# The last down projection of a hybrid attention kernel: exact 12-bit parts in place of float32

## The chip, the core and the metric

One core of one Trainium2 chip runs the whole kernel in one launch. The metric is the device time of the launch in microseconds; the median of some runs is given. The core has five engines that run side by side, each with its own queue of instructions that it takes in order: TensorE (PE, the matrix unit; PEld is its weight load), VectorE (DVE), ScalarE (ACT), GpSimd (POOL) and SyncE (SP, which here only issues DMAs). Tiles live in SBUF; matmuls write to PSUM, which has eight banks of 128 partitions by 512 float32.

## The reference

The input `x` has 4 images of 512 rows by 256 columns. Three layers run one after the other, each adding to `x`:

- Layer a, a windowed attention. An image is seen as 8192 tokens of 16 channels on a grid of 128 by 64; query, key and value come from a 16x48 matrix. Half of the channels attend in windows of 1x8, half in windows of 8x1, each with a depthwise 3x3 convolution added, then a projection, a layer norm and the residual.
- A feed-forward layer (called f below): layer norm over 256 columns, then `down(gelu(gate(x)) * up(x))` with 2048 hidden units, and the residual.
- Layer b, a causal attention with 16 heads of 16 over the 512 rows, with rotary embedding; then the same feed-forward layer again (called s below), with the same weights, and the residual.

The gate, up and down weights are 4-bit codes with scales, two codes in a word, dequantised once in the kernel to float32.

## The kernel before

The work of one feed-forward pass over one image is the unit to keep in mind: f0 to f3 and s0 to s3. The hidden units go through in 16 chunks of 128. For each chunk `n` TensorE makes a gate tile `pg` and an up tile `pu` (128 hidden units by 512 rows, one PSUM bank each), ScalarE applies the gelu, VectorE multiplies them to `it`, and after eight chunks (a `half`) the down projection runs: for each of 4 groups `i` of 128 rows, eight float32 matmuls of 256 columns into a bank `po`, which VectorE adds to the image's tile `X[b]`.

From f2 on, gate and up products don't run in float32. Each operand is split into a high part of 12 bits and a rest; `keep_parts` writes three forms of the gate and up weights (high; the rest; a third one for the correction) to a tensor in device memory, `kept`. For each weight tile ScalarE makes three scaled copies (`less`, `high`, `low`), SP stores them, and GpSimd issues two accumulating DMAs that add a tile onto what was stored: a first stage `kept<-raw` onto the `less` form, and two turns later a second stage `kept<-kept`, which reads what the first stage left. So each turn is three activations, three stores and two accumulating DMAs. Then a gate or up tile takes four products in a fast float32 form, a scaling of the bank by 1 + 2^-12 on ScalarE, and two more products onto it (`begin` and `end`). The chunks come back from `kept` by one DMA of 768 KB each (`chunk_f`, `chunk_s`).

What sets the order:

- The first part (windowed attention of the four images, f0 to f2) is woven by hand: `weave` takes steps of a feed-forward pass and of the window work beside it. It holds TensorE's order, and in the weave of f1 GpSimd's; the other engines' instructions are placed by the framework's scheduler, which may put them earlier than written. `beside_window(2)` is the window work of image 2, beside f1, with `keep_parts` in between; `beside_window(3)` stands beside f2. Each ends with `norm_rows`, which makes the normed and turned rows `xT` of the next feed-forward pass; its `inv_root` runs on GpSimd and gives `rs_f`.
- The second part (causal attention of the four images, f3 and s0 to s3) is ordered by a planner, the class `Conductor`: every step has an engine, a cost in us and a rank, and the planner writes out all engines' orders. `RANK`, `BOOST` and the number given to `run` are its tuning. s3 stands alone at the end, as nothing is left to run beside it.
- PSUM: two double banks (`pair`), and in the first part one bank `one` and three banks `fbank` (tag `ps`), in the second part four `ps`.

Of the kernel before, what the change touches and what calls it, by code (L numbers as in the profile page):

```python
# [18 lines left out]
P = 128  # L19
# [20 lines left out]
def hybrid_kernel(  # L40
# [47 lines left out]
    X = [const.tile([P, 4, W], F32, name=f"X{b}") for b in range(B)]  # L88
# [19 lines left out]
    store = ctx.enter_context(tc.tile_pool(name="store", bufs=1, space=bass.MemoryType.DRAM))  # L108
    kept = [store.tile([4, P, 2, 3, 2, P], F32, name=f"kept{q}") for q in range(4)]
# [852 lines left out]
    def down(b, name, half, inter, last, later=None):  # L962
        for i in range(4):
            if later:
                later.room()
            po = fbank.tile([P, 512], F32, tag="ps", name=f"po_{name}_{half}_{i}")
# [34 lines left out]
    def keep_parts(pool):  # L1001

        of = lambda t: t.rearrange("p (n c) -> p n c", c=P)
        turns = [(q, k, mat, par) for q in range(4) for k, mat in enumerate("gu") for par in range(2)]

        def home(at, form):
            q, k, _, par = turns[at]
            return kept[q][:, :, k, form, par, :].rearrange("n p c -> p n c")

        for at in range(len(turns) + 4):  # L1010
            if at < len(turns):
                q, k, mat, par = turns[at]
                w = Wf[mat][par][q]
                less = pool.tile([P, 512], F32R, tag="g2", name=f"less_{mat}{par}_{q}")
                high = pool.tile([P, 512], F32R, tag="gu", name=f"high_{mat}{par}_{q}")
                nc.scalar.activation(less, w, AF.Copy, scale=-NEAR)
                nc.sync.dma_start(out=home(at, 1), in_=of(less.bitcast(F32)))
                nc.scalar.activation(high, w, AF.Copy, scale=NEAR)
                nc.sync.dma_start(out=home(at, 0), in_=of(high.bitcast(F32)))
                low = pool.tile([P, 512], F32, tag="g2", name=f"low_{mat}{par}_{q}")  # L1020
                nc.scalar.activation(low, high.bitcast(F32), AF.Copy, scale=-STEP)
                nc.sync.dma_start(out=home(at, 2), in_=of(low))
            if 0 <= at - 2 < len(turns):
                q, k, mat, par = turns[at - 2]
                nc.gpsimd.dma_start(out=home(at - 2, 1), in_=of(Wf[mat][par][q]), accum_op=ALU.add)
            if 0 <= at - 4:
                nc.gpsimd.dma_start(out=home(at - 4, 2), in_=home(at - 4, 1), accum_op=ALU.add)
            yield 0.0

# [11 lines left out]
    def ffn_in_parts(pool, ipool, ring, b, xT, name, tanh, last):  # L1041

        xs = in_parts(ring, xT, name)
        chunks = {}

        def begin(mat, n):
# [3 lines left out]
            ps = fbank.tile([P, 512], F32, tag="ps", name=f"p{mat}_{name}_{n}")  # L1050
# [14 lines left out]
        for half in range(2):  # L1065
# [38 lines left out]
            for _ in down(b, name, half, inter, last):  # L1104
                yield 0.86
# [21 lines left out]
    HOLD, BOOST = 0.25, 6.1  # L1127

    class Conductor:
# [9 lines left out]
            max=-2.21, oT=1.96, gu=0.59, add=4.1, parts=2.85, norm_s=-1.04, inv=-2.33, qb=1.22, v=1.99,  # L1139
            straight=2.4, sum=-0.69, norm_b=3.15, cube=3.78, it=8.4, plane=1.98, exp=3.03, scale=-1.64, copy=1.69,  # L1140
            gelu=0.87, square=2.39, tanh=2.67,
# [133 lines left out]
    def conduct(ring, got3, got_b0):  # L1275
# [67 lines left out]
        def ffn_pass(b, name, xT, tanh, last):  # L1343
# [33 lines left out]
            def end(mat, n):  # L1377
# [27 lines left out]
                else:  # L1405
                    gs, g2 = tiles.pop(("gate", n))
                    it = inter[n] = Slot(II, [P, 512], F32, "it", f"it_{name}_{n}")
                    if tanh:
                        gu = Slot(PF, [P, 512], F32, "gu", f"gu_{name}_{n}")
# [4 lines left out]
                    else:  # L1414
                        step("DVE", 0.69, lambda: nc.vector.tensor_tensor(it(), ps(), gs(), ALU.mult),
                             r=[ps, gs], w=[it], new=[it], lane="ffn", rank="gu")

            def down(half, i):
# [14 lines left out]
                final = b == B - 1 and last and half == 1 and i == 3  # L1433
                parts = 2 if final else 1
                for n in range(parts):
                    at = slice(n * W // parts, (n + 1) * W // parts)
                    step("DVE", 0.42 / parts, lambda at=at: nc.vector.tensor_tensor(X[b][:, i, at], po()[:, at], X[b][:, i, at], ALU.add),  # L1437
                         r=[po], w=[("X", b, i)], lane="ffn", rank="add")
                    if last and half == 1:
                        step("ACT" if n else "SP", 0.06,  # L1440
                             lambda at=at, n=n: (nc.scalar if n else nc.sync).dma_start(out=out[b, i * P : (i + 1) * P, at], in_=X[b][:, i, at]),
                             r=[("X", b, i)], lane="ffn", rank=6)

            seq = [(mat, n) for n in range(16) for mat in ("g", "u")]
            held = None
            for k, (mat, n) in enumerate(seq):
                if (mat, n) == ("g", 8):
# [11 lines left out]
                held = mat, n  # L1459
            end(*held)  # L1460
# [7 lines left out]
        def consts():  # L1468
# [9 lines left out]
            sq = [bc.tile([P, 4, HEADS, 32], F32, name=f"sq{i}") for i in range(2)]  # L1478
            sk = [bc.tile([P, HEADS, 32], F32, name=f"sk{i}") for i in range(4)]
            V = bc.tile([P, 4, HEADS, 32], F32, name="V")  # L1480
# [113 lines left out]
        qT = bc.tile([P, 4, 512], F32, name="qT")  # L1594
        kT = bc.tile([P, 4, 512], F32, name="kT")
# [311 lines left out]
    with ExitStack() as left:  # L1907
# [216 lines left out]
        def beside_window(b):  # L2124
# [8 lines left out]
            yield from between(beside, keep_parts(f1) if b == 2 else iter(()))  # L2133
# [22 lines left out]
        weave(ffn_in_parts(f1, i1, wraw, 2, got[2], "f2", False, False), beside_window(3), 1.0)  # L2156
# [4 lines left out]
    with tc.manual_schedule(  # L2161
# [5 lines left out]
        conduct(ring, got[3], mine[0]).run(0.068)  # L2167
# [88 lines left out]
```

## Time and profile before

| | us |
|---|---|
| median of 3 runs | 993.89 (990.49 to 994.48) |
| the profiled execution, its own time | 989.58 |
| its span in the profile | 987.9 |
| TensorE busy | 950.0 (96%) |
| VectorE busy | 698.5 (71%) |
| ScalarE busy | 489.6 (50%) |
| GpSimd busy | 178.7 (18%) |

A row of the profile has the line in the code, the engine, the operation, what it writes and reads by the program's names, the shapes and a count. In a timeline the first two numbers are the start and the length in us; in brackets stands the idle time of the engine before the row and what ended it. A float32 matmul stands as two records, a product from parts as one. TensorE's records overlap, because matmuls are pipelined, so the cost of one is read from start to start. f1 runs from about 187 to 285 us, f2 from there to 373 us, and s3 from 912 us to the end. TensorE's clock is granted in full nearly everywhere (mean 0.991).

### The profile page before, as it was taken

How to read it: one execution, taken by the hardware profiler on the slowest of the kernel's cores; microseconds unless marked ns; L12 is line 12 of the kernel's file. 1: busy time of each engine (PE TensorE's matmuls, PEld its weight loads, DVE VectorE, ACT ScalarE, POOL GpSimd, SP SyncE). 2: the span in 40 equal slices, each digit the busy share in tenths (PEclk: the TensorE clock that was granted, in tenths of full speed). 3: DMA queues.
4: the chain of work that ended last, by engine and by line, in shares of the span. 5: the costliest groups of instructions: out<-in, count | busy, mean ns of one | idle time of the engine just before them, and what ended most of it. 6: DMA issues, size and time to landing. Idle time of an engine off the chain costs nothing.

```text
span 987.9 us, 15864 instructions
## 1 busy us (share of the span) xinstructions
PE 950.0 (96%) x5936; PEld 662.5 (67%) x5936; DVE 698.5 (71%) x1598; ACT 489.6 (50%) x872; POOL 178.7 (18%) x295
## 2 busy tenths in 40 slices
PE   8989998899999999899999999999999999999998
PEld 6864657555677776666566666676666667657887
DVE  8999996889794868865876676667776667556211
ACT  4562277541334423565462853737717648475531
POOL 2100000078200024111422123111141111120000
PEclk9999998999999999999999999999999999999999
DMA  5320147799916325421220330522503406134730
GB/s 144 97 66 22 64 116 203 208 120 194 155 47 209 128 60 201 137 89 65 97 97 1 128 129 7 187 75 83 185 1 128 139 15 220 35 133 139 255 126 31
DMA packets 70975, 111.92 MB, mean 113 GB/s; under 512 B 5682, under 2 KB 55114, under 8 KB 70866
## 3 DMA queue, kind: packets, MB, share of 16 engines
q1 hardware_dynamic: 52000, 101.92, 31.7%
q0 software_dynamic: 16992, 8.44, 7.2%
q8 instruction: 47, 0.77, 0.3%
q10 hardware_dynamic: 1906, 0.54, 0.3%
q14 instruction: 30, 0.25, 0.1%
HBM read 92.01 MB, written 23.07 MB: 116 GB/s over the span
## 4 chain that ended last, share of the span: by engine, by line
PE 76%; DVE 12%; ACT 5%; DMA 3%; issue 1%; SPq 1%; POOL 0%; DVEq 0%; ACTq 0%
PE po_s L1425 11%; PE pg_s L1369 6%; PE pu_s L1369 6%; PE pg_f L925 5%; PE pu_f L946 5%; PE s L1640 5%; PE po_f L974 4%; PE sT L1674 4%; PE o L1718 3%; PE pu_s L1382 3%; PE po_f L1425 3%; PE qk_b L1553 3%; PE pg_s L1382 3%; PE v_b L1585 2%; PE pg_f L1369 2%; DMA chunk_f<-kept 1%
## 5 line engine op out<-in xcount | busy, mean ns | idle before, releaser
L1654 DVE CUSTOM_DVE_ANT_0 junk<-s,mask 128x512 f32<-128x512 f32 (+3 forms) x256 | 125.6, 491 | 54.3 <-PE s L1640 20.7
L1425 PE MATMUL po_s<-d,it_s 128*128 128x256 f32 x512 | 117.7, 382 | 0.6 <-DVE it_s L1412 0.5
L1693 POOL TENSOR_SCALAR_AFFINE_SELECT e<-e 128x256 f32<-128x256 f32 x128 | 53.4, 429 | 340.0 <-ACT e L1686 314.2
L1425 PEld LDWEIGHTS po_s<-d,it_s 128*128 128x128 f32 x512 | 95.2, 190 | 20.5 <-issue 5.2
L1686 ACT ACTIVATE e<-sT 128x1024 f32<-128x1024 f32 (+1 forms) x66 | 64.7, 1006 | 88.7 <-PE sT L1674 88.6
L974 PE MATMUL po_f<-d,it_f 128*128 128x256 f32 x384 | 86.4, 381 | 1.0 <-DVE it_f L1091 0.6
L974 PEld LDWEIGHTS po_f<-d,it_f 128*128 128x128 f32 x384 | 71.8, 190 | 12.6 <-issue 1.1
L1369 PE MATMUL pg_s<-xs_s,chunk_s 128*128 128x512 f32 x256 | 71.5, 401 | 0.5 <-ACT qT L1617 0.5
L1369 PE MATMUL pu_s<-xs_s,chunk_s 128*128 128x512 f32 x256 | 71.3, 400 | 0.5 <-DVE gu_s L1410 0.5
L1369 PEld LDWEIGHTS pu_s<-xs_s,chunk_s 128*128 128x128 f32 x256 | 47.6, 190 | 18.2 <-issue 1.7
L1374 ACT ACTIVATE pu_s<-pu_s 128x512 f32<-128x512 f32 x64 | 37.3, 583 | 42.1 <-PE pu_s L1369 41.2
L1369 PEld LDWEIGHTS pg_s<-xs_s,chunk_s 128*128 128x128 f32 x256 | 47.5, 190 | 14.9 <-ACT qT L1617 1.3
L937 ACT ACTIVATE gs_f<-pg_f 128x512 f32<-128x512 f32 x32 | 19.0, 594 | 73.9 <-PE pg_f L925 71.0
L1640 PE MATMUL s<-kT,qT 16*128 16x256 f32 (+3 forms) x512 | 50.9, 468 | 3.2 <-ACT qT L1617 1.9
L1374 ACT ACTIVATE pg_s<-pg_s 128x512 f32<-128x512 f32 x64 | 37.3, 583 | 22.1 <-PE pg_s L1369 21.6
L1396 DVE SCALAR_TENSOR_TENSOR g_s<-g_s,gs_s 128x512 f32<-128x512 f32 x48 | 33.6, 701 | 20.5 <-ACT g_s L1394 20.5
L1718 PE MATMUL o<-e,V 128*32 128x256 f32 (+3 forms) x512 | 44.4, 442 | 0.0
L1410 DVE SCALAR_TENSOR_TENSOR gu_s<-pu_s,gs_s 128x512 f32<-128x512 f32 x48 | 33.0, 689 | 14.7 <-PE pu_s L1382 13.9
L1382 PE MATMUL pu_s<-xs_s,chunk_s 128*128 128x512 f32 x128 | 41.8, 408 | 1.1 <-ACT pu_s L1374 1.1
L1382 PE MATMUL pg_s<-xs_s,chunk_s 128*128 128x512 f32 x128 | 41.8, 408 | 0.3 <-ACT pg_s L1374 0.3
L1437 DVE TENSOR_TENSOR X<-po_s,X 128x256 f32<-128x256 f32 (+1 forms) x33 | 13.3, 413 | 35.9 <-PE po_s L1425 35.9
L946 PE MATMUL pu_f<-xT_f,raw 128*128 128x512 f32 x80 | 38.6, 594 | 0.0
(317 smaller groups left out, 1951.4 us busy)
## 6 DMA issues: line engine op xcount, KB each, us to landing
chunk_s<-kept SPq DMA_DIRECT2D x64, 768.0 KB
chunk_f<-kept SPq DMA_DIRECT2D x32, 768.0 KB
kept<-kept POOLq DMA_DIRECT2D x16, 256.0 KB, 6.9
kept<-raw POOLq DMA_DIRECT2D x9, 256.0 KB, 7.8
X<-in_x_dram SPq DMA_DIRECT2D x4, 512.0 KB
kept<-less_g SPq DMA_DIRECT2D x8, 256.0 KB
kept<-high_g SPq DMA_DIRECT2D x8, 256.0 KB
kept<-low_g SPq DMA_DIRECT2D x8, 256.0 KB
```

The costliest lines, as they stand in the source:

```text
L925: nc.tensor.matmul(pg, Wf["g"][par][q][:, o : o + P], xT[:, par, :], start=par == 0, stop=par == 1)
L946: nc.tensor.matmul(pu, Wf["u"][par][q][:, o : o + P], xT[:, par, :], start=par == 0, stop=par == 1)
L974: nc.tensor.matmul(po[:, 0:W], inter[k][:, i * P : (i + 1) * P], Wf["d"][par][j // 2][:, (j % 2) * W : (j % 2 + 1) * W], start=k == 0, sto ...
L1369: nc.tensor.matmul(ps(), ch()[:, int(mat == "u"), form, par], xs()[:, form, par], start=k == 0, stop=k == 3)
L1374: step("ACT", 0.585, lambda: nc.scalar.activation(ps(), ps(), AF.Copy, scale=1.0 + STEP), r=[ps], w=[ps], lane="ffn", rank="scale")
L1382: nc.tensor.matmul(ps(), ch()[:, int(mat == "u"), 2, par], xs()[:, 2, par], start=False, stop=par == 1, skip_group_check=True,)
L1425: nc.tensor.matmul(po()[:, 0:W], inter[n]()[:, i * P : (i + 1) * P], Wf["d"][par][j // 2][:, (j % 2) * W : (j % 2 + 1) * W], start=k == 0, ...
L1640: nc.tensor.matmul(pss[hl // 2]()[:, hl % 2, p0 : p0 + n], qT[h0 : h0 + HD, g, i * P : (i + 1) * P], kT[h0 : h0 + HD, g, 0:n], start=True, ...
L1654: step("DVE", 0.155 + n / 960.0 + 0.085, lambda hl=hl, i=i, p0=p0, n=n, h=h, junk=junk: nc.vector.tensor_tensor_reduce(out=junk()[:, 0:n], ...
L1686: step("ACT", 0.16 + 2 * total / 1200.0, lambda: nc.scalar.activation(e()[:, :, 0:total], pss[k]()[:, :, at0:512], AF.Exp), r=[(pss[k], "t ...
L1693: nc.gpsimd.affine_select(out=diag, in_=diag, pattern=[[0, 2], [1, P]], compare_op=ALU.is_ge, fill=0.0, base=0, channel_multiplier=-1,)
L1718: nc.tensor.matmul(o()[h0 : h0 + 32, kt * P : 512], c["V"][:, kt, 4 * g + hl, :], e()[:, hl % 2, p0 : p0 + n], start=kt == 0, stop=kt == 2,)
```

## The change

- The last pass s3 makes its down projection from parts too. Chunks 0 to 14 of `it` are split by two activations and two subtractions into `high`, `low` and a third form; chunk 15 stays in float32. The projection runs in four quarters of four chunks (`down_parts`), each some chunks after its inputs: for each row group `down_open` makes two products per chunk, ScalarE scales the bank (`half`), and `down_close` adds the third product per chunk.
- The parts live in room that the causal attention has left: the third form in the tiles of `qT` and `kT`, `high` and `low` in those of `it` and `e`, and the down weights' parts, loaded by SP in 16 DMAs, in those of `sq0`, `sq1`, `V` and two images `X`.
- `keep_parts` takes a list of turns. `keep_gate_up` does what was done before beside f1, and `keep_down` makes the eight tiles of down weights' parts, called in the window work beside f2. GpSimd's order is held in that weave too.
- In f2 every fourth PSUM tile comes from the bank `one`, so that four banks turn.
- `BOOST`, all of `RANK` and the lead of the planner have other values.

```diff
+    kept_d = [store.tile([2, P, 2, 3, W], F32, name=f"kept_d{q}") for q in range(4)]
...
-            po = fbank.tile([P, 512], F32, tag="ps", name=f"po_{name}_{half}_{i}")
+            po = bank(name_) if bank else fbank.tile([P, 512], F32, tag="ps", name=name_)
...
+    def keep_parts(pool, turns):
         for at in range(len(turns) + 4):
             if at < len(turns):
+                w, home, of, name = turns[at]
...
                 nc.scalar.activation(less, w, AF.Copy, scale=-NEAR)
+                nc.sync.dma_start(out=home(1), in_=of(less.bitcast(F32)))
                 nc.scalar.activation(high, w, AF.Copy, scale=NEAR)
+                nc.sync.dma_start(out=home(0), in_=of(high.bitcast(F32)))
...
                 nc.scalar.activation(low, high.bitcast(F32), AF.Copy, scale=-STEP)
+                nc.sync.dma_start(out=home(2), in_=of(low))
             if 0 <= at - 2 < len(turns):
+                w, home, of, name = turns[at - 2]
+                nc.gpsimd.dma_start(out=home(1), in_=of(w), accum_op=ALU.add)
             if 0 <= at - 4:
+                home = turns[at - 4][1]
+                nc.gpsimd.dma_start(out=home(2), in_=home(1), accum_op=ALU.add)
             yield 0.0
+    def keep_down(pool):
+        def home(q, par):
+            return lambda form: kept_d[q][par][:, :, form]
+        of = lambda t: t.rearrange("p (j c) -> p j c", c=W)
+        return keep_parts(pool, [(Wf["d"][par][q], home(q, par), of, f"d{par}_{q}") for q in range(4) for par in range(2)])
...
+        def bank(name):
+            count[0] += 1
+            return one(name) if count[0] % 4 == 0 else fbank.tile([P, 512], F32, tag="ps", name=name)
...
-            ps = fbank.tile([P, 512], F32, tag="ps", name=f"p{mat}_{name}_{n}")
+            ps = bank(f"p{mat}_{name}_{n}")
...
-    HOLD, BOOST = 0.25, 6.1
+    HOLD, BOOST = 0.25, 8.94
...
+                        it = Slot(PF, [P, 512], F32, "gu", f"it_{name}_{n}")
                         step("DVE", 0.69, lambda: nc.vector.tensor_tensor(it(), ps(), gs(), ALU.mult),
                              r=[ps, gs], w=[it], new=[it], lane="ffn", rank="gu")
+                        if n == 15:
+                            inter[n] = it
+                            return
...
+                        step("ACT", 0.63, lambda: nc.scalar.activation(at(high), it(), AF.Copy, scale=NEAR),
+                             r=[it], w=[high], lane="ffn", rank="high", **first)
+                        step("DVE", 0.69, lambda: nc.vector.tensor_tensor(room(), it(), f(high), ALU.subtract),
+                             r=[it, high], w=[key], lane="ffn", rank="low")
+                        step("ACT", 0.63, lambda: nc.scalar.activation(at(low), room().bitcast(F32), AF.Copy, scale=4096.0),
+                             r=[key], w=[low], lane="ffn", rank="times", **then)
+                        step("DVE", 0.69, lambda: nc.vector.tensor_tensor(room(), f(high), f(low), ALU.subtract),
+                             r=[high, low], w=[key], lane="ffn", rank="diff")
...
+            def down_open(q, i):
+                if i == 0:
+                    for par in range(2):
+                        load(q, par)
...
+                ns = range(4 * q, min(4 * q + 4, 15))
+                def go():
+                    for k, (n, form) in enumerate((n, form) for n in ns for form in range(2)):
+                        nc.tensor.matmul(
+                            po()[:, 0:W], inter[n][4](inter[n][form])[:, i * P : (i + 1) * P],
+                            chunks["d", q, n % 2, n // 2 % 2][0]()[:, form], start=k == 0, stop=k == 2 * len(ns) - 1,
+                        )
...
+                step("ACT", 0.37, lambda: nc.scalar.activation(po()[:, 0:W], po()[:, 0:W], AF.Copy, scale=1.0 + STEP),
+                     r=[slot], w=[slot], lane="ffn", rank="half")
+            def down_close(q, i):
...
+                    for n in ns:
+                        nc.tensor.matmul(
+                            po()[:, 0:W], inter[n][2]()[:, i * P : (i + 1) * P],
+                            chunks["d", q, n % 2, n // 2 % 2][0]()[:, 2], start=False, stop=n == ns[-1], skip_group_check=True,
+                        )
...
+            def down_rest(i):
...
+                    po()[:, 0:W], inter[15]()[:, i * P : (i + 1) * P], Wf["d"][1][3][:, W : 2 * W],
...
-            yield from between(beside, keep_parts(f1) if b == 2 else iter(()))
+            yield from between(beside, keep_gate_up(f1) if b == 2 else keep_down(f1))
...
-        weave(ffn_in_parts(f1, i1, wraw, 2, got[2], "f2", False, False), beside_window(3), 1.0)
+        weave(ffn_in_parts(f1, i1, wraw, 2, got[2], "f2", False, False), beside_window(3), 1.0, PE_ONLY | {mybir.EngineType.Pool})
...
-        conduct(ring, got[3], mine[0]).run(0.068)
+        conduct(ring, got[3], mine[0]).run(0.062)
```

## The prediction

> **What bounds the kernel now.** I read the page's busy shares and slices first, then the chain of waits, then the timelines of the stretches that the change touches.
>
> ```profile
> PE 950.0 (96%) x5936; PEld 662.5 (67%) x5936; DVE 698.5 (71%) x1598; ACT 489.6 (50%) x872; POOL 178.7 (18%) x295
> L1425 PE MATMUL po_s<-d,it_s 128*128 128x256 f32 x512 | 117.7, 382 | 0.6 <-DVE it_s L1412 0.5
> L1425 PEld LDWEIGHTS po_s<-d,it_s 128*128 128x128 f32 x512 | 95.2, 190 | 20.5 <-issue 5.2
> ```
>
> TensorE is busy 96% and idle for some 12 us in all between 375 and 950 us. Only fewer TensorE cycles, or fewer of its waits, shorten the span. A float32 matmul stands as two records, so 512 records are 256 matmuls. The next view is TensorE's timeline at the end (start, length, what).
>
> ```profile
> 966.83 1.07 PE L1369 MATMUL pg_s<-xs_s,chunk_s 128*128 128x512 f32 x4
> 967.73 0.61 PE L1382 MATMUL pu_s<-xs_s,chunk_s 128*128 128x512 f32 x2
> 968.19 1.07 PE L1369 MATMUL pu_s<-xs_s,chunk_s 128*128 128x512 f32 x4
> 969.93 0.73 PE L1382 MATMUL pu_s<-xs_s,chunk_s 128*128 128x512 f32 x2 [0.22 <-ACT pu_s L1374]
> 970.49 13.98 PE L1425 MATMUL po_s<-d,it_s 128*128 128x256 f32 x64
> ```
>
> Start to start, six products from parts take 968.19 - 966.83 = 1.36 us, 0.227 us each at 512 columns. The last 32 down matmuls take 13.83 us (the chain's figure for them; the row's 13.98 holds the end of the last), 0.432 us each at 256 columns. Nothing hides this stretch. The third view is the boundary of passes f1 and f2, on GpSimd, VectorE, TensorE and ScalarE.
>
> ```profile
> 240.73 1.26 POOL L1027 DMA_DIRECT2D kept<-kept  x1 [0.84 <-issue]
> 241.49 1.82 POOL L1025 DMA_DIRECT2D kept<-raw  x1
> 253.14 1.26 POOL L1027 DMA_DIRECT2D kept<-kept  x1 [4.40 <-issue]
> 255.49 1.26 POOL L1027 DMA_DIRECT2D kept<-kept  x1 [1.09 <-DMA kept<-raw]
> 259.17 1.25 POOL L1027 DMA_DIRECT2D kept<-kept  x1 [2.42 <-issue]
> 270.34 0.19 POOL L114 TENSOR_SCALAR rs_f<-mv_f 128x4 f32<-128x4 f32 x1 [9.91 <-DVE mv_f L861]
> 271.69 1.39 DVE L878 TENSOR_SCALAR xn_f<-X,mv_f,rs_f 128x256 f32<-128x256 f32 x4 [1.44 <-POOL rs_f L115]
> 285.33 1.30 DVE L1036 TENSOR_TENSOR xs_f<-xT_f,xs_f 128x512 fp32r<-128x512 f32 x2
> 286.74 1.10 PE L1052 MATMUL pg_f<-xs_f,chunk_f 128*128 128x512 f32 x2 [0.89 <-ACT xs_f L1037]
> 231.63 0.60 ACT L937 ACTIVATE gs_f<-pg_f 128x512 f32<-128x512 f32 x1 [11.63 <-PE pg_f L925]
> ```
>
> GpSimd issues 32 accumulating DMAs from 205 us, the last at 259.17. Then it is free, and the inverse root `rs_f` of pass f2 runs at 270.34 as soon as its variance is there. From 271.69 to 285.33 VectorE is full, and TensorE's f2 matmuls wait at its end: this boundary lies on the chain of waits.
>
> **The last pass.** Per row group 15 of 16 hidden chunks become three products from parts each: 15 x 4 x 3 = 180 matmuls of 256 columns; chunk 15 stays float32, 4 matmuls. Removed: 64 x 0.432 = 27.65 us. No row shows a product from parts at 256 columns. The near end: eight transposes, each with a weight load and 128 columns, in 0.87 us.
>
> ```profile
> 214.17 1.04 PE L390 MATMUL yTp<-ident,xa 128*128 128x128 f32 x8
> 215.04 1.02 PE L946 MATMUL pu_f<-xT_f,raw 128*128 128x512 f32 x2
> ```
>
> That is 0.109 us. The far end is a weight load that nothing hides, 0.190 us by the LDWEIGHTS row. I take half of 0.227, rounded up, 0.115: the 512-column products hide their load almost wholly, and the transposes show that loads follow each other every 0.109. So 180 x 0.115 + 4 x 0.432 = 22.4 us; saved 5.2. The closing products wait for ScalarE's scaling, as the row at 969.93 does (0.22); two such places stand bare instead of one, so 5.0. The ends: 6.1 us saved at 0.109, 8.3 us lost at 0.190.
>
> The Trainium skill, page "TensorE: Matmul & The Clock Gate", sections "LDWEIGHTS (loading the stationary operand)" and "What overlaps and what doesn't", speaks against this step: a load of 128 columns takes 128/1.2 = 107 ns and overlaps a running matmul only in another row group, by which 180 x 0.213 + 1.7 = 40 us would stand in place of 27.7, 12 us lost. The trace disagrees at 512 columns, where load and product together take 0.227.
>
> Cover in that pass: ScalarE has 16 x 1.77 us now, and gets 30 x 0.63 and 16 x 0.37, 53 us beside TensorE's 16 x 2.72 + 22.4 = 66; VectorE gets 30 x 0.69 more and stays under 40. The chain of one chunk's parts is 5 steps, 3.3 us; a quarter opens two chunks (5 us) later, and the last one behind 5.6 us of the third quarter's products. If that cover is gone, one chain, some 3 us, stands bare. The 16 loads of 384 KB stand on SP behind buffers freed quarters earlier, between the chunk loads; both draw 18.9 MB in 66 us, 286 GB/s, where gates and ups alone draw 0.786 MB per 2.72 us, 289, without a wait of TensorE.
>
> **The parts of the down weights.** They are written beside f2, but the order of the changed program as built puts them elsewhere: nothing pins ScalarE and SP, so the 24 activations follow those of the gate and up weights, from before gelu 2 of f1 to before gelu 8. The 24 stores stand on SP before f2's first chunk load (issued at 241 us, needed at 286: covered). All 16 new accumulating DMAs stand on GpSimd ahead of f2's `rs_f`. Behind that wait: xn on VectorE, behind it 13.6 us of window products and then `xs_f`, and TensorE for those.
>
> GpSimd's new queue: one new DMA stands early (+1.0 us: 256 runs of 1 KB, between 0.64 us for an issue of 128 runs and 1.83 for 512), the other first-stage ones begin after the row at 255.49. The issue of a second stage waits for the landing of its own first stage, with the first stages of two more turns ahead of it, so three turns take one landing L plus 0.8 us. From the second turn's first stage at A the queue is free at A + 3L + 2.4. A is 255.5 + 0.8 + 1.0 = 257.3 if the stores leave the old 32 alone; they add 16 stores where the queue is already landing-bound, so I add 3 us (0 to 6): 260.3. For L the rows give
>
> ```profile
> kept<-kept POOLq DMA_DIRECT2D x16, 256.0 KB, 6.9
> kept<-raw POOLq DMA_DIRECT2D x9, 256.0 KB, 7.8
> DMA to landing us min/median/max: 4.7/6.9/10.6
> ```
>
> With half as many runs and a queue that empties I take 5.5, nearer the minimum: free at 260.3 + 16.5 + 2.4 = 279.2, 8.9 us late. One product of 1.1 us moves ahead of `xs_f` on VectorE: TensorE starts f2 10.0 us late. The ends: 257.3 + 14.1 + 2.4 = 273.8, 4.6 us late; with L = 9 and 260.3, 20.5 us late.
>
> The Trainium skill's page "DMA: Bandwidth & Descriptors", section "Anatomy of one DMA — SWDGE (gpsimd) path", gives 2.0 us plus bytes/436e3, 2.6 us for 256 KB, by which the delay would be about nil. These DMAs took 4.7 at the least, so the rows decide.
>
> ScalarE delays f1 too: a turn waits for its stores, about 2.4 us apart from landing at 189 to 199 us, 4 us if the accumulating traffic doubles it. Then gelu 8 (231.63) is some 7 us late, where TensorE has three banks, 3.4 us, of room: 4 us (0 to 9). That is inside the 10 us, as both shift the same boundary, and the later one counts.
>
> **The fourth bank of f2.** TensorE's waits for a free bank in f2, from the list of waits, are 0.8, 0.7 and 0.5 us. I count -1.5 (0 to -2). GpSimd's order moves f3's `rs_f` ahead of the memsets (368.75 now, its variance is there 1 us earlier): -0.5 (0 to -1).
>
> **The new ranks, BOOST and lead.** They reorder the attention stage, not its work. TensorE's longest waits in it are 1.9, 1.7 and 0.7 us; I take 0, bounds -3 and +3.
>
> The sum: -5.0 + 10.0 - 1.5 - 0.5 = +3.0. The profiled execution took 989.58 (span 987.9, 1.7 around it), so it would be 992.6. It is 4.3 below the median of 993.89, which becomes 997. Runs of this kernel differ by 0.4%, so 0.5%, 5 us, is about what tells a change from none.
>
> **Rivals.** First, the queue catches up: DMAs with half the runs land in under 4 us, GpSimd is free by 271, and 7 us stay gained, less up to 2: 987 to 989. For it: the 10 us of idle time before 270.34; against it: no accumulating DMA landed under 4.7. Second, slower: landings stay at 9 us, as the last three of the old queue did (241.49 to 253.14 is 11.6 from issue to release), so the boundary is 20.5 us late: 20.5 - 7 = +13.5, 1007. It decides above L = 6.2, where the sum passes +5. For it: ScalarE's stores and f2's chunk loads share the same engines; against it: both are over when the last turns run. Third, also slower: weight loads bound the new products, 0.190 each: +3.0 + 13.3 = +16, 1010; the transposes speak against it.
>
> **Chances.** The delay of about 10 us: 0.55 (0.35 of it within 0.5%, 0.20 above). The queue catches up: 0.27 (0.20 faster, 0.07 within). Landings at 9 us: 0.13. Loads bound: 0.05. So faster 0.20, within 0.5% 0.42, slower 0.38. The forecast's own range is 992 to 1003; to hold 8 in 10 it goes from 987, the first rival, to 1008, past the second.
>
> **What would show it.** In the profile after: `rs_f` of f2 near 280 us with GpSimd's DMAs directly ahead, and a wait of TensorE of some 10 us at f2's first products; three 256-column products in about 0.345 us in the last pass, which takes 5 us less. `rs_f` at 271 or products at 0.19 us would prove the sum wrong.

## The result, and the profile after

The changed kernel takes 1005.11 us (median of 6 runs, 1003.92 to 1011.24), the kernel before on the same chip 993.01 (987.07 to 994.79): ratio 1.0148, 95% interval 1.0106 to 1.0189. It is 1.5% slower. The profiled execution took 1004.31 us with a span of 1002.6, 14.7 more than the 987.9 of before. Other chips ran the experiments; each is compared with the kernel before by a ratio from its own chip.

The page after: the busy shares, the chain of waits by engine, and one group of f1.

```profile
PE 947.5 (95%) x5996; PEld 662.3 (66%) x5996; DVE 719.8 (72%) x1636; ACT 526.9 (53%) x944; POOL 197.7 (20%) x311
...
PE 71%; DMA 10%; DVE 9%; ACT 5%; issue 2%; POOL 2%; SPq 1%; DVEq 0%; ACTq 0%; POOLq 0%
...
L947 PE MATMUL pu_f<-xT_f,raw 128*128 128x512 f32 x80 | 42.0, 640 | 14.7 <-ACT gs_f L938 9.7
```

TensorE has less work than before (950.0) and a longer span: the loss is waiting. DMAs and GpSimd now hold 12% of the chain (3% and 0% before), and f1's up products, which waited 0.0 us in the same group of before, wait 14.7, 9.7 of it for a gelu. The starts of the same instructions in both timelines place the loss:

| first record of | before | after | later by |
|---|---|---|---|
| f1's gate products | 187.23 | 188.83 | 1.6 |
| window products behind f1's gates (`aTp`) | 246.15 | 266.82 | 20.7 |
| f2's products, second group | 286.74 | 316.66 | 29.9 |
| f3's transposes | 373.03 | 401.18 | 28.2 |
| s3's transposes | 899.25 | 916.03 | 16.8 |
| end of the span | 987.9 | 1002.6 | 14.7 |

So 29.9 us were lost before f2's products, and half of it came back later. Of the 29.9, 1.6 stood before f1 already; runs whose code up to there is that of the kernel before start f1 at 187.23, 188.69 (e11) and 190.01 us (e4), so 1.6 is within the spread of runs. Counted from f1's first gate product, f2's second group comes after 99.5 us before and after 127.8 now. The boundary in the timeline after, on ScalarE, VectorE, TensorE and GpSimd:

```profile
234.14 0.63 ACT L1010 ACTIVATE less_d<-d 128x512 fp32r<-128x512 f32 x1 [3.86 <-DMA kept_d<-less_d]
248.50 0.63 ACT L1010 ACTIVATE less_d<-d 128x512 fp32r<-128x512 f32 x1 [4.67 <-DMA kept_d<-less_d]
252.37 1.08 ACT L938 ACTIVATE gs_f<-pg_f 128x512 f32<-128x512 f32 x2
...
225.16 1.08 DVE L609 TENSOR_REDUCE sm<-ek 128x64 f32<-128x512 f32 x1 [6.70 <-ACT ek L604]
...
238.26 3.37 PE L947 MATMUL pu_f<-xT_f,raw 128*128 128x512 f32 x4 [5.03 <-DVE X L991]
253.02 3.78 PE L947 MATMUL pu_f<-xT_f,raw 128*128 128x512 f32 x4 [9.68 <-ACT gs_f L938]
316.66 1.39 PE L1070 MATMUL pg_f<-xs_f,chunk_f 128*128 128x512 f32 x2 [1.70 <-ACT xs_f L1051]
...
272.22 1.66 POOL L1019 DMA_DIRECT2D kept_d<-d  x1
298.20 0.88 POOL L1022 DMA_DIRECT2D kept_d<-kept_d  x1 [1.62 <-issue]
299.16 0.20 POOL L115 TENSOR_SCALAR rs_f<-mv_f 128x4 f32<-128x4 f32 x1
```

Two queues stand full. On ScalarE the last down turns come 7 us apart, each waiting for the stores of the one before it to free its tiles, and f1's gelu 8 stands behind the last of them: 252.37, where before it ran at 231.63. VectorE's window work stands behind the same turns by way of the activation `ek` (a wait of 6.70 us at 225.16; 1.35 us in the kernel before), and TensorE's wait of 5.03 us for VectorE most likely follows from it. On GpSimd the new accumulating DMAs end at 299, and `rs_f` follows without idle time, 28.8 us later than before.

The late products are slow as well. The windows of the timeline after, from 230 to 262 us (busy time of PE, PEld, DVE, ACT, POOL; granted clock; DMA share; GB/s):

```profile
230.00:249.00 19.00, 8.32 (x19) 3.62 (x17) 11.24 (x16) 3.92 (x7) 11.49 (x9) 0.88 1.32 223
249.00:262.00 13.00, 8.98 (x15) 3.90 (x16) 9.00 (x12) 3.72 (x6) 8.22 (x7) 0.65 1.39 201
```

The group behind 253.02, and a group of four such records in the kernel before:

```profile
256.60 2.66 PE L926 MATMUL pg_f<-xT_f,raw 128*128 128x512 f32 x4
...
231.43 1.88 PE L946 MATMUL pu_f<-xT_f,raw 128*128 128x512 f32 x4
```

The group at 253.02 takes 3.78 us where four such records took 1.88 before: half speed, after a wait of 9.68 us. With the groups at 238.26 (3.37) and 256.60 (2.66) the clock cost (3.37 + 3.78 + 2.66) - 3 x 1.88 = 4.2 us. The Trainium skill's page "TensorE: Matmul & The Clock Gate", section "The HAM clock gate", says that the clock falls to half after an idle window of some 3.4 us; these rows agree.

Eight products of the new down projection in the last pass, in TensorE's timeline:

```profile
949.75 0.29 PE L1512 MATMUL po_s<-sq_parts,high_s 128*128 128x256 f32 x1
...
949.99 0.40 PE L1512 MATMUL po_s<-sq_parts,both_s 128*128 128x256 f32 x2
...
950.69 1.09 PE L1387 MATMUL pg_s<-xs_s,chunk_s 128*128 128x512 f32 x4
```

Between 949.75 and 950.69 stand only these products of 256 columns, eight of them: 0.1175 us each, weight load and product together.

### The profile page after: what moved, and what is told of

Its sections match the earlier page's. It is cut to its first block, busy times and chain, and to the rows that moved or that the text cites. A ratio compares the mean times of both kernels' runs of the same rounds, so it can differ in the third digit from the quotient of the medians.

```text
span 1002.6 us, 16192 instructions
## 1 busy us (share of the span) xinstructions
PE 947.5 (95%) x5996; PEld 662.3 (66%) x5996; DVE 719.8 (72%) x1636; ACT 526.9 (53%) x944; POOL 197.7 (20%) x311
## 4 chain that ended last, share of the span: by engine, by line
PE 71%; DMA 10%; DVE 9%; ACT 5%; issue 2%; POOL 2%; SPq 1%; DVEq 0%; ACTq 0%; POOLq 0%
PE po_s L1468 8%; PE pg_s L1387 6%; PE pu_s L1387 6%; PE s L1785 4%; PE po_f L976 4%; PE o L1863 4%; PE sT L1819 4%; DMA kept<-raw 3%; PE pu_s L1400 3%; PE qk_b L1692 3%; PE pg_s L1400 3%; PE pg_f L926 3%; PE po_f L1468 3%; PE pu_f L947 3%; DMA kept_d<-d 2%
## 5 line engine op out<-in xcount | busy, mean ns | idle before, releaser
L1831 ACT ACTIVATE e<-sT 128x1024 f32<-128x1024 f32 (+1 forms) x66 | 65.0, 1007 | 96.6 <-PE sT L1819 96.5
L1468 PE MATMUL po_s<-d,it_s 128*128 128x256 f32 x384 | 90.3, 384 | 0.9 <-DVE it_s L1430 0.9
L1468 PEld LDWEIGHTS po_s<-d,it_s 128*128 128x128 f32 x384 | 70.7, 190 | 19.3 <-issue 7.3
L947 PE MATMUL pu_f<-xT_f,raw 128*128 128x512 f32 x80 | 42.0, 640 | 14.7 <-ACT gs_f L938 9.7
L1392 ACT ACTIVATE pg_s<-pg_s 128x512 f32<-128x512 f32 x64 | 37.4, 584 | 20.5 <-PE pg_s L1387 19.6
L938 ACT ACTIVATE gs_f<-pg_f 128x512 f32<-128x512 f32 x32 | 18.9, 594 | 55.2 <-PE pg_f L926 52.2
L1819 PE MATMUL sT<-qT,kT 17*128 17x512 f32 (+3 forms) x392 | 38.5, 480 | 0.3 <-ACT qT L1762 0.3
## 6 DMA issues: line engine op xcount, KB each, us to landing
kept<-kept POOLq DMA_DIRECT2D x16, 256.0 KB, 10.3
kept<-raw POOLq DMA_DIRECT2D x9, 256.0 KB, 11.7
```

What stands on the lines that cost most here:

```text
L947: nc.tensor.matmul(pu, Wf["u"][par][q][:, o : o + P], xT[:, par, :], start=par == 0, stop=par == 1)
L1392: step("ACT", 0.585, lambda: nc.scalar.activation(ps(), ps(), AF.Copy, scale=1.0 + STEP), r=[ps], w=[ps], lane="ffn", rank="scale")
L1468: nc.tensor.matmul(po()[:, 0:W], inter[n]()[:, i * P : (i + 1) * P], Wf["d"][par][j // 2][:, (j % 2) * W : (j % 2 + 1) * W], start=k == 0, ...
L1819: nc.tensor.matmul(pss[hl // 2]()[:, hl % 2, p0 : p0 + n], kT[h0 : h0 + HD + 1, g, kt * P : (kt + 1) * P], qT[h0 : h0 + HD + 1, g, kt * P ...
L1831: step("ACT", 0.16 + 2 * total / 1200.0, lambda: nc.scalar.activation(e()[:, :, 0:total], pss[k]()[:, :, at0:512], AF.Exp), r=[(pss[k], "t ...
```

## The experiments

Two theories stood at first. The two queues: the new work costs time only where it stands, ScalarE's turns in f1 and GpSimd's DMAs ahead of `rs_f`. The rival: the transfers and turns cost the same wherever they stand.

### e1: no accumulating DMAs for the down weights

```diff
-            if 0 <= at - 2 < len(turns):
+            if adds and 0 <= at - 2 < len(turns):
...
-            if 0 <= at - 4:
+            if adds and 0 <= at - 4:
```

> The changed kernel without the 16 accumulating DMAs that finish the down weights' parts (their sums are left out; the 24 activations and 24 stores stay). In the changed kernel f2's first products from parts come 29.9 us later than before (316.66 against 286.74): some 19 us are there when the first projection matmuls of f1 run (266.82 against 246.15), the rest comes after. Theory A, two queues: ScalarE's turns wait for their stores beside the gate and up accumulations, which stay, so the 19 us stay; GpSimd is free for f2's inverse root early, so the last 9 us go: 9 us less than the changed kernel, some 996. Rival B, the bytes: the accumulating DMAs of the down parts themselves slow the stores, so without them most of the 30 us go: under 985.

Measured: 997.75 us (995.25 to 999.21), ratio 1.0072 (1.0054 to 1.0091). The timeline of e1, on ScalarE, GpSimd and TensorE:

```profile
250.32 1.08 ACT L938 ACTIVATE gs_f<-pg_f 128x512 f32<-128x512 f32 x2
288.43 0.20 POOL L115 TENSOR_SCALAR rs_f<-mv_f 128x4 f32<-128x4 f32 x1 [12.81 <-DVE mv_f L862]
305.95 1.40 PE L1070 MATMUL pg_f<-xs_f,chunk_f 128*128 128x512 f32 x2 [2.00 <-ACT xs_f L1051]
```

GpSimd waits for data again, not `rs_f` for GpSimd, and f2's products come 10.7 us earlier. Gelu 8 is still 18.7 us late, where it was 20.7: the last turns stay 7 us apart without the down weights' own accumulations. What is left beside their stores is the traffic of the gate and up weights; that this slows the stores is likely, but no run takes it away.

### e2: the 24 stores alone

```diff
+            if plain:
+                if at < len(turns):
+                    w, home, of, name = turns[at]
+                    for form in range(3):
+                        nc.sync.dma_start(out=home(form), in_=of(w))
+                yield 0.0
+                continue
```

> The changed kernel in which the down parts are not made: SP stores the float32 weight three times in their place (24 stores, no activation, no accumulating DMA; what the last pass multiplies is not the parts). As built these stores stand on SP ahead of most of the gate and up stores. Theory A: the whole delay of 30 us at the start of f2 goes, and what is left is the gain of the rest: the last pass (4 us), the planner's new order (some 9 us from f2's end to the last pass) and f2's bank (2 us), so 993 - 15 = 978, and gelu 8 of f1 stands at about 232 us as before. Rival B: 6.3 MB of stores alone cost several us by their traffic wherever they stand: 983 to 990.

Measured: 980.79 us (979.52 to 987.39), ratio 0.9919 (0.9893 to 0.9946). f2's second group is at 292.80, and f1's first gate product at 193.30; in e4, without the stores, they are at 289.51 and 190.01. From there to f2's second group it takes 99.5 us in both, as in the kernel before. So the stores cost nothing in f1; ahead of f1 they cost 3.3 us against e4, or 6.1 against the kernel before (these two start f1 2.8 us apart, with the same code up to there). The time lies between the two expectations. The bytes are cheap; the waits behind the turns and sums are not.

### e3: the turns queued beside f2

```diff
+                low_behind = pin and last_on(mybir.EngineType.Activation).name
-                nc.scalar.activation(less, w, AF.Copy, scale=-NEAR)
+                ins = nc.scalar.activation(less, w, AF.Copy, scale=-NEAR)
+                if pin:
+                    queue_behind(ins, low_behind)
```

and the same for `high`.

> The changed kernel with one thing more: the first two activations of each turn of the down parts stand behind the ScalarE instruction that was written last before them, so the turns run beside f2, as the change says, and not beside f1. GpSimd's accumulating DMAs then stand behind f2's inverse root. Theory A, two queues: the 30 us at f2's start go; f2 pays something, because its chunk loads share SP with stores that wait for ScalarE (0 to 8 us): 978 to 986, faster than before. Rival B, the bytes or the turns cost the same wherever they stand: f2 is longer by 15 us or more and the time stays at 993 or above.

Measured: 1000.06 us (996.96 to 1007.85), ratio 1.0104 (1.0049 to 1.0159). The theory of the two queues missed: f1 and the boundary are whole again (f2's second group at 289.29), but f2 takes 114.7 us from transposes to transposes where e4 has 94.3. ScalarE's and TensorE's timeline of e3:

```profile
330.88 0.63 ACT L1011 ACTIVATE less_d<-d 128x512 fp32r<-128x512 f32 x1 [5.63 <-DMA kept_d<-less_d]
348.12 1.22 PE L1083 MATMUL pg_f<-xs_f,chunk_f 128*128 128x512 f32 x2 [9.28 <-ACT pg_f L1078]
```

The same jam in another pass: activations of four turns stand on ScalarE between gelu 7 and the scaling of `pg_f` 8, most of them waiting for stores. A better place had to be one where no wait stands ahead of path work.

### e4: the new ranks, boost and lead alone

```diff
-    HOLD, BOOST = 0.25, 6.1
+    HOLD, BOOST = 0.25, 8.94
-            max=-2.21, oT=1.96, gu=0.59, add=4.1, parts=2.85, norm_s=-1.04, inv=-2.33, qb=1.22, v=1.99,
+            max=-1.96, oT=1.66, gu=-0.5, add=5.93, parts=3.86, norm_s=2.11, inv=1.36, qb=2.77, v=3.29,
...
-        conduct(ring, got[3], mine[0]).run(0.068)
+        conduct(ring, got[3], mine[0]).run(0.062)
```

> The kernel before with the new ranks, BOOST and lead of the planner alone. By the traces the stretch from f2's end to the end of s2 is some 9 us shorter in the changed kernel. Theory A: that is the new order, so 993 - 9 = 984. Rival: the order is tuned for a last pass that this kernel does not have, or the 9 us come from a clock that was not throttled there (0.93 from 373 to 425 us before, 1.00 after): 990 to 996.

Measured: 994.46 us (992.1 to 997.22), ratio 1.0034 (1.0015 to 1.0053). No gain in all, but not for lack of effect: from f3's transposes to those of s0 it takes 161.7 us where before took 169.0, and from s0's to s1's 137.2 where before took 130.1. The reading at that point, that the order is worth nothing, was wrong, as e11 shows.

### e5: as e3, with the stores on ScalarE's own DMA queue

```diff
-                nc.sync.dma_start(out=home(1), in_=of(less.bitcast(F32)))
+                (nc.scalar if pin else nc.sync).dma_start(out=home(1), in_=of(less.bitcast(F32)))
```

and the same for the other two.

> The changed kernel with the first two activations of each down turn queued behind the last ScalarE instruction written so far (so the turns run beside f2, as in e3) and, new here, the three stores of a turn issued from ScalarE's own DMA queue and not from SP. In e3 f2 stayed 20 us too long: at 348.12 a pair of products waited 9.3 us for an activation that stood behind turns waiting for their stores, and seven chunk loads and stores stood in SP's queue in turn. Theory one, a ring of waits through SP's queue (store behind chunk load, chunk load behind TensorE, TensorE behind ScalarE, ScalarE behind the store): stores that no longer pass SP take it away, f2 lasts about as in e4 (94 us from first transposes to those of f3), and the time is 980 to 987. Theory two, the landing of the stores and the two slots of a tile are the limit wherever they are issued: pg_f 8 still waits over 5 us and the time stays at 994 to 1002.

Measured: 1006.99 us (1005.9 to 1009.01), ratio 1.0156 (1.0116 to 1.0196), with the wait unchanged in its timeline:

```profile
347.76 0.63 ACT L1011 ACTIVATE less_d<-d 128x512 fp32r<-128x512 f32 x1 [3.52 <-DMA kept_d<-less_d]
350.83 1.22 PE L1083 MATMUL pg_f<-xs_f,chunk_f 128*128 128x512 f32 x2 [9.11 <-ACT pg_f L1078]
```

The ring through SP's queue falls. Theory two's wait is there, but the time lies above its range: f2 takes 120.1 us from transposes to transposes, 5.4 more than in e3. That the 24 issues on ScalarE cost this is likely and not shown.

### e6: f2's inverse root on VectorE

```diff
-        if aside is None:
+        if aside is None and name == "f2":
+            newton_root(rs, mv[:, :, 1], pool.tile([P, 4], F32, tag="rt", name=f"rt_{name}"), 1.0)
+        elif aside is None:
             inv_root(rs, mv[:, :, 1])
```

> The changed kernel with only f2's inverse root taken from GpSimd and made on VectorE by the kernel's own Newton steps (nine small instructions), so that f2's beginning no longer stands behind the 16 new accumulating DMAs in GpSimd's queue; all DMAs still run. If it is the place in the queue that cost the 9 to 11 us which e1 gave back, f2's first products come at 304 to 308 and the time is 994 to 998. If the transfers themselves cost it, whoever waits, the time stays at 1002 to 1006.

Measured: 998.95 us (997.41 to 1004.43), ratio 1.0077 (1.0049 to 1.0106), as e1, though all 16 DMAs run. TensorE's timeline:

```profile
308.56 1.40 PE L1072 MATMUL pg_f<-xs_f,chunk_f 128*128 128x512 f32 x2 [2.00 <-ACT xs_f L1053]
```

8.1 us earlier than in the changed kernel (time and start lie just above the first expectation): it is the place in GpSimd's queue that costs most of what e1 gave back. The other 2.6 us of e1's 10.7 can be the transfers, as gelu 8 is 2 us earlier there and not here (252.12). The rest of the delay is the 24 activations': e1 and e2 differ by them, and from f1's first gate product to f2's second group it takes 127.8 us in the changed kernel, 120.2 in e6, 117.2 in e1 and 99.5 in e2.

### e7: f2 with three banks

```diff
-            return one(name) if count[0] % 4 == 0 else fbank.tile([P, 512], F32, tag="ps", name=name)
+            return fbank.tile([P, 512], F32, tag="ps", name=name)
```

> The changed kernel with f2's products in three PSUM banks again. By the prediction the fourth is worth 1.5 us (0 to 2): 1005 to 1007. The rival, that it is worth nothing because f2 begins with ScalarE and GpSimd late anyway: 1003 to 1005.5.

Measured: 1009.37 us (1008.84 to 1014.59), ratio 1.0195 (1.0142 to 1.0248), above both expectations. In its trace f2 takes 101.6 us from transposes to transposes (changed kernel 100.1), the 1.5 us foreseen. The rest lies ahead of f2, whose transposes already stand 3.0 us later, where this edit changes nothing; the intervals overlap, so the total tells the bank's worth no closer. Where f2 is not disturbed more shows: e10 and e2, with four banks, take 91.4 and 91.0 us from transposes to transposes, e4 and e11, with three, 94.3 and 94.8. That is some 3.3 us for the bank and GpSimd's order together, which no run separates.

### e8: the changed kernel with the old ranks, boost and lead

```diff
-    HOLD, BOOST = 0.25, 8.94
+    HOLD, BOOST = 0.25, 6.1
...
-        conduct(ring, got[3], mine[0]).run(0.062)
+        conduct(ring, got[3], mine[0]).run(0.068)
```

and the old `RANK`, with the five new kinds kept.

> The changed kernel with the conductor's ranks, boost and lead of the kernel before (the five new kinds of step keep their new ranks). By the prediction the ranks are worth nothing (0, up to 3 either way): 1002 to 1008. The rival from the traces, that the new order is what brings f3's transposes to those of the next stage from 169 to 161.5 us, and the last stages with it: 1009 to 1016.

Measured: 1023.15 us (1020.25 to 1025.55), ratio 1.0315 (1.0272 to 1.0359): worse than either expectation, 17 us above the changed kernel's ratio. From s0's transposes to s1's it takes 138.3 us, the bump of e4 again, though e4 has the other ranks. What e4 and e8 share is a mix of old and new. That pointed at the planner: it compares what is done in TensorE's two lanes with their whole cost, the last pass is in that sum, and so a change at the end shifts the order from f3 on. e11 and e12 take that apart.

### e9: sums in SBUF by GpSimd, turns beside f2

```diff
+                if own:
+                    nc.gpsimd.tensor_tensor(less.bitcast(F32), less.bitcast(F32), w, ALU.add)
...
+                if own:
+                    nc.gpsimd.tensor_tensor(low, low, less.bitcast(F32), ALU.add)
...
-            if 0 <= at - 2 < len(turns):
+            if not own and 0 <= at - 2 < len(turns):
```

on top of e3; the second stage goes too.

> As e3 (the down turns' activations queued beside f2, stores from SP), but without the 16 accumulating DMAs of the down weights: GpSimd adds the two sums of a turn in SBUF (two tensor_tensor of 128x512, some 1.6 us each from the 0.81 us of a 128x256 one) before the part is stored. In e3 and e5 the store of one part took 4 to 8 us until its landing released the next turn's tile, and pg_f 8 waited 9 us for ScalarE behind four such turns. If the accumulating traffic makes the landings slow, they come down to 2.5 to 4 us, pg_f 8 waits under 4 us, and the time is 982 to 989. If it is the two slots and the place beside f2's gate and up products, whatever the traffic, the time stays at 993 to 1002.

Measured: 996.01 us (993.3 to 1001.72), ratio 1.0074 (1.0049 to 1.0098). Half an answer. The wait for ScalarE came down as the first expectation said:

```profile
339.66 1.22 PE L1087 MATMUL pg_f<-xs_f,chunk_f 128*128 128x512 f32 x2 [3.76 <-ACT pg_f L1082]
```

but f2 still takes 108.1 us, 14 more than in e4. Of e3's 20 us, 6.6 went with the accumulating DMAs. The rest stays with the place beside f2; how much of it is the two slots of a tile and how much a ScalarE that f2 needs was not separated.

### e10: the parts made later, in the ring of chunks

```diff
+        def keep_down_turn():
+            q, par = kept_turns.pop(0)
+            t = Slot(RING, [P, 2, 3, W], F32R, "chunk", f"parts_d{par}_{q}")
...
+            step("POOL", 1.5, lambda: nc.gpsimd.tensor_tensor(plain(1), plain(1), w, ALU.add),
+                 w=[(t, 1)], lane="ffn", rank=6.0)
...
+            step("SP", 4.0, lambda: nc.sync.dma_start(out=kept_d[q][par], in_=t().bitcast(F32)),
+                 r=[(t, 0), (t, 1), (t, 2)], w=[("kept_d", q, par)], lane="ffn", rank=1)
...
+                    if (name, n) in (('f3', 8), ('f3', 9), ('s0', 8), ('s0', 9), ('s1', 8), ('s1', 9), ('s2', 8), ('s2', 9)):
+                        keep_down_turn()
...
-            yield from between(beside, keep_gate_up(f1) if b == 2 else keep_down(f1))
+            yield from between(beside, keep_gate_up(f1) if b == 2 else iter(()))
```

> The changed kernel with the down weights' parts made neither in f1 nor in f2: two turns stand before chunks 8 and 9 of each of the passes f3, s0, s1 and s2, in the conductor's order; a turn fills one slot of the ring of chunks (6 KB a partition) by three activations and two GpSimd additions, and one store of 768 KB writes it. Nothing of it stands in a queue that f1 or f2 waits for, and there are no accumulating DMAs for it. By the theory of the two queues f1 and f2 go as in e4 (f2's first products at 286 to 290, f3's transposes at 373 to 376), the later passes go as in the changed kernel (601 us from f3's transposes to the end), and the time is 976 to 983: faster than both kernels. By the rival, that the turns cost the same wherever they stand (24 activations of 0.63 us, 8 slots of the ring), the later passes get 15 to 20 us longer and the time is 992 or more.

Measured: 979.39 us (976.46 to 981.61), ratio 0.9878 (0.9851 to 0.9905): 1.2% faster than the kernel before, 2.7% faster than the changed one by the two ratios (its chip's two medians alone, 979.39 and 989.42, differ by 1.0%). The timeline of e10 at the boundary:

```profile
272.74 0.20 POOL L115 TENSOR_SCALAR rs_f<-mv_f 128x4 f32<-128x4 f32 x1 [10.69 <-DVE mv_f L862]
289.13 1.10 PE L1070 MATMUL pg_f<-xs_f,chunk_f 128*128 128x512 f32 x2 [0.88 <-ACT xs_f L1051]
```

and the rows of the tile that a turn fills:

```profile
L1335 POOL TENSOR_TENSOR parts_d<-parts_d,d x8: 1292/1297/1403, 411.6 to 835.1; 128x512 f32<-128x512 f32 x8
L1341 POOL TENSOR_TENSOR parts_d<-parts_d x8: 1264/1331/1647, 416.0 to 838.5; 128x512 f32<-128x512 f32 x8
```

All 24 activations and 6 MB of stores are there, spread from 411 to 840 us; the sums are GpSimd's and not accumulating DMAs. From f3's transposes to s3's it takes 518.1 us against 514.9 in the changed kernel: all eight turns cost 3.2 us, where in f1 they cost some 28. The rival falls. Two things changed at once, the place and the sums; but e9 has the sums on GpSimd too and takes 108.1 us for f2, where e10 takes 91.4, so the place counts for most of it. Turns with accumulating DMAs in the later passes were not tried.

### e11: the new order with the old last pass

```diff
-            whole["ffn"] *= 0.8
+            whole["ffn"] = 0.8 * (whole["ffn"] - 27.68 + 22.612)
```

on top of e4.

> The kernel before (float32 last pass, nothing of the down weights' parts) with the new ranks, boost and lead as in e4, and one number more: the planner weighs the two lanes of TensorE by their whole cost, into which the last pass enters (64 products of 0.865/2 us, against 22.6 us of the new pass); here that sum is given the value it has in the changed kernel. With it TensorE's order of f3 to s2 is that of the changed kernel, instruction by instruction, and only the last pass differs, so this run and e10 stand apart by the last pass alone. If the new order is what made the passes from f3 to s2 shorter (before 614.9 us from f3's transposes to the end, changed 601.4) and the last pass gives only 2 to 5 us, as its rows say, the time is 981 to 986. If the gain is the last pass's, the time is 989 to 994, that of the kernel before.

Measured: 982.66 us (982.38 to 984.95), ratio 0.9928 (0.9905 to 0.995). From f3's transposes to s3's 516.0 us, where before took 526.2: 10.2 us. Some 1.8 of that is only moved: in the new order eight more records of s2's down projection (four float32 matmuls) stand behind s3's transposes, and from those to s3's first products it takes 14.8 us instead of 13.0. So the new order alone is worth 8.4 us up to s3's first products. TensorE's matmul records from f3's to s3's transposes have the same tiles in the same sequence as in the changed kernel, all 3730. From s3's transposes to the end 90.7; e10, with the new pass and the same order but for two records, takes 86.5: the last pass is worth 4.2. (e10 differs from e11 in more than the last pass, namely the turns, f2's banks and GpSimd's order, so only this stretch is compared and not the times.)

### e12: the old order with the new last pass

```diff
-            whole["ffn"] *= 0.8
+            whole["ffn"] = 0.8 * (whole["ffn"] + 27.68 - 22.612)
```

on top of e8.

> The counterpart: the changed kernel with the old ranks, boost and lead as in e8, and the planner's sum given the value it has in the kernel before, so that TensorE's order of f3 to s2 is that of before, instruction by instruction, and the last pass is the new one. It keeps the changed kernel's late f1 and f2. If the new order is worth 7 to 11 us, the time is 1011 to 1016; e8's 1023 then held 7 us or more from the planner's shifted sum. If the order is worth nothing by itself, the time is 1003 to 1007.

Measured: 1013.98 us (1012.59 to 1017.87), ratio 1.0243 (1.0207 to 1.0279). From f3's transposes to s3's 525.9 us, as before (526.2), with the same 3738 records in the same sequence. From s3's transposes to the end it takes 85.9 us, where before took 88.65: in the old order the last pass is worth 2.8. By the ratios of e12 and the changed kernel the order is worth 0.0243 - 0.0148 = 0.95%, 9.4 us; the other 7 us of e8's loss came with the planner's shifted sum.

## Why the prediction was right and wrong

The time, 1005.1, lies inside the range of 987 to 1008, but outside the forecast's own 992 to 1003, and close to the second rival's 1007; it is slower by over 0.5%, which had a chance of 0.38. That it lies inside is luck: it got there by two large errors of opposite sign, a boundary sized 20 us too small and an order that was put at nothing, and not by that rival's sum. By steps:

- **The f2 boundary, +10.0 (4.6 to 20.5): it was +29.9.** The mechanism was right, and so was the reading that ScalarE and GpSimd shift the same boundary and the later one counts: e6 takes GpSimd away and 8.1 us come back, and nearly all that is left goes with the activations (e2). Both terms were mis-sized. GpSimd's queue was free at 299.1 and not at 279.2. The formula A + 3L + 2.4 holds: the second turn's first stage stands at A = 272.2 (foreseen 260.3), which asks for L = 8.2 (foreseen 5.5), and the median landing of the first stages was 8.4. The landing times of the DMAs on `kept_d` in the changed kernel, the first line for the first stages (median), the second for both stages:

```profile
kept_d<-d POOLq DMA_DIRECT2D x8, 256.0 KB, 8.4
...
DMA to landing us min/median/max: 4.4/7.6/9.4
```

  The 3 us added for the stores in the old queue should have been 15: the old second stages on `kept` landed in 10.3 us and not in 6.9, in the median. The figure of the Trainium skill's page "DMA: Bandwidth & Descriptors", section "Anatomy of one DMA — SWDGE (gpsimd) path", some 2.6 us for 256 KB, was further off still.
- **ScalarE in f1, 4 us (0 to 9) inside the 10: it was 19.1** (20.7 less the 1.6 that stood before f1). Turns were assumed 4 us apart; they came 7 us apart, so gelu 8 was not some 7 us late but 20.7. TensorE then waited 5.0 and 9.7 us and lost 4.2 to the clock, which the sum had not counted at all: together 18.9. This is the step that failed most. The estimate doubled a landing of 2.4 us from a stretch ahead of the accumulating DMAs, and each tile has two slots only. The DMA share where the late turns stand is 1.32, and it was 1.36 in the kernel before from 230 to 249 us, so the load of the place could be read ahead.
- **The ranks, 0 (-3 to +3): -8 to -10.** The step argued from TensorE's waits, which are small. From f3's transposes to the end it takes 614.9 us before, 606.7 with the new order alone (e11), 611.7 with the new last pass alone (e12) and 601.4 with both: the order gives 8.2 us with the old pass and 10.3 with the new one. In time e11 shows 7 us against the kernel before and e12 9.4 against the changed one. By the starts in e11 the gain lies mostly in the first stretch: f3's transposes to s0's take 162.7 us for 169.0, s0 to s1 129.6 for 130.1, s1 to s2 129.7 for 130.9, s2 to s3 94.0 for 96.3 (the last of these holds the 1.8 us that only moved). TensorE's granted clock in 375 to 425 us also goes from 0.93 to 0.97, which over 50 us is an estimated 2 us of the first stretch's 6.3.
- **The last pass, -5.0 (-6.1 to +8.3): -4.2** between e11 and e10, -2.8 between the kernel before and e12. The product took 0.1175 us, not 0.115, which makes 0.45 us of the difference. The rest of the difference has no run. The Trainium skill's page "TensorE: Matmul & The Clock Gate", section "What overlaps and what doesn't", lets a weight load overlap a running matmul only in another row group; by it the pass was estimated at 40 us in place of 27.7. Neither this nor the third rival holds here: product and load together take 0.1175. In the plain difference of the two profiles only 2.1 us show after s3's transposes (88.65 to 86.57), because the new order puts more of s2's down projection behind those transposes (90.7 in e11).
- **The fourth bank, -1.5: -1.5** in f2's length (e7); GpSimd's order at f3, -0.5, can't be told apart. In an undisturbed f2 both together give 3.3 (e10 and e2 against e4 and e11), more than the 2.0 foreseen.

The stretches of the profile then sum to: +29.9 at the boundary, -1.7 in f2, -11.4 from f3 to s3, -2.1 in s3: +14.7. With the boundary at the 10 us foreseen it would have been about -5 (an estimate from these stretches); e10, where the parts cost 3.2 us, shows the gain.

## What to carry to other kernels

Ask of added background work not how much it is, but what stands behind it in each queue that it passes: eight turns cost 28 us in front of a gelu and an inverse root, and, with their sums on GpSimd, 3 us in a stage with room. A chain of write, wait for landing, write again runs at the landing time under the load of its place, which is read from the DMAs there, not from quiet ones. And where a planner orders the work, a change at the end changes the order from the start: hold the planner's inputs fixed, as e11 and e12 do, before a gain is put down to the new code.

## What was not expected of the hardware

- A TensorE wait of 5 to 10 us cost more than the wait: the products after it ran at down to half speed (3.78 us for 1.88), with a granted clock of 0.65 over 13 us.
- The stores of 256 KB let a turn follow only 7 us later where the DMA share is 1.32, beside the accumulating DMAs of the gate and up weights, with or without accumulations of its own (e1); ahead of the accumulating DMAs turns followed each other 3 us apart (kernel before, 188.8 to 197.9 us).
- GpSimd adds two tiles of 128x512 in SBUF in 1.3 us. Issuing one of the accumulating DMAs on `kept` holds it for 1.26 or 1.83 us, and its landing took 10.3 or 11.7 us in the median, 6.9 or 7.8 before the change.
